# Seeding a PSUM bank with ScalarE's copy of product one instead of adding a snapshot, in a seven-product matmul kernel

## The chip, the cores and the metric

The kernel runs on one core of one Trainium2 chip, in fp32 throughout. The metric is the device time of one execution in microseconds (us). TensorE (PE) does the matmuls and writes PSUM; VectorE (DVE), ScalarE (ACT) and GpSimd (POOL) do the rest; SyncE (SP) issues nearly all DMAs. Each engine works through a queue of its own, in the order in which the built program put its instructions there.

## The reference, cut to what matters

`x` is (8, 512, 512); the feed-forward width is 2048. Linear attention and a gated feed-forward run on the same normalized tokens, and the one gates the other:

```python
xn = layernorm(x)
q, k, v = xn @ Wq.T + bq, xn @ Wk.T + bk, xn @ Wv.T + bv
s = ((elu(q) + 1) * cumsum((elu(k) + 1) * v, axis=1) * 32 ** -0.5) @ Wo.T + bo
h = fwht(xn * SU_ug) / 64                      # Walsh-Hadamard transform
h = silu(h @ W_gate.T * (Wscale_ug[2048:] * 64)) * (h @ W_up.T * (Wscale_ug[:2048] * 64))
y = (fwht(h * SU_dp) / 64) @ W_down.T * (Wscale_dp * 64)
out = x + s * silu(y)
```

## The kernel before, in words

**Seven products for a matmul.** A product of two 2x2 block matrices is made from seven block products instead of eight (Strassen's scheme in Winograd's form), of operands that were added up beforehand (`encode_tokens`, `encode_weights`). The seven are P1 to P7; in the code their indices are `P1, P2, P7, P3, P4, P5, P6 = range(7)`, so a tile called `gu_1_0_3` is pair 1, hidden unit 0, outer product with index 3, which is P3. The four outputs are sums of them, and most of the summing happens in PSUM: bank `px` takes P1, then P6, P5 and P3 onto it; bank `pz` takes P7, then P4. Between the steps a copy of `px` is read away.

- Output 1 = P1 + P2. Before: `px` after P1 is read to SBUF (snapshot `sa`), P2 goes to a bank of its own, `py`, and VectorE adds the two.
- Output 2 = (P1 + P6) + P4 and output 4 = (P1 + P6 + P5) + P7: snapshots `sb` and `sc`, each added to `pz` by VectorE.
- Output 3 = `px` after P3, read directly.

PSUM's eight banks are three `px`, one `py`, two `pz` and two `t` (L447).

**Three recorders** write this order out:

- `group` (L450), for k, v, q (24 times in all) and, in the first pair, gate and up (12 times). A source matmul has 512 columns and shows as two passes; a product has two such matmuls. Snapshots are ScalarE's, with the bias added.
- `token_groups` (L520), for the attention's output projection `o` (4 times) and the down projection `dn` (8 times). It runs two groups of rows, g = 0 and 1, side by side. Where something has to be added (a bias, or the first half of `dn`), the read of `px` is a VectorE addition (L547), else a ScalarE copy (L545).
- `block_product` (L630), for a hidden unit's gate and up together (`gu`), 91 times. This is a second level: a hidden unit is itself seven outer products P1, P5, P6, P2, P7, P3, P4 (`hidden_unit`, L810 on), each a `block_product` of seven inner products of two 128x256 source matmuls. The reads of `px` are plain ScalarE copies for the outer P1 and P5 (L646, L674) and VectorE additions onto an earlier outer result for the others (L648, L676). The addition for output 1 is L657, that of the last inner product L680.

**The order of the work** is written out with an agenda: `at(place, fn)` puts a step at a place, `advance(n)` runs what is due. A `block_product` puts its steps at places 0 P1, 2 P2, 3 P7, 4 P6, 8 P5, 12 P3, 13 P4, and advances by 7, so that the last three fall between the first four of the next block, at its places 1, 5 and 6. The order on PE is therefore P1, previous P5, P2, P7, P6, previous P3, previous P4. `group` does the same with places in units of a product. A scheduler then places the instructions on the engines' queues, waits included, by priority; it can move an instruction of one engine past another where nothing depends on it.

**The stages.** Four pairs p of batch entries: attention (k, v, q for each of two groups of heads), then four hidden units u; `o` follows u = 0, `dn` follows u = 1 (first half) and u = 3 (second half, whose outputs go through Silu, L882, a product on POOL, L883, and an addition, L884). In pair 0 the first three units use `group` with weights that are folded on the chip meanwhile (`folded_w` L946-952, `fold_down` L998-1004), so VectorE and ScalarE have much more to do there; 13 units go through `hidden_unit`: u = 3 of pair 0 and all of pairs 1 to 3.

**The end of a hidden unit.** With outer P7 done, POOL adds its result `r` to `v` in two halves (L842, in `with_r`), ScalarE puts each half through Silu (L828, in `gated`), and POOL multiplies (L829). Outer P3 and P4 follow on PE meanwhile.

Of the kernel before, what the change touches and what calls it, by code (L numbers as in the profile page):

```python
# [8 lines left out]
F32 = mybir.dt.float32  # L9
AF = mybir.ActivationFunctionType  # L10
# [11 lines left out]
def kernel(  # L22
# [66 lines left out]
    def pace(ins, us):  # L89
        while us > 0 and (urgent or idle):  # L90
            t, fn, args = (urgent or idle).pop(0)
            with tc.issue_after(ins.ins):
                fn(*args)
            us -= t
# [24 lines left out]
    su_ug = const.tile([P, KD], F32, tag="su_ug", name="su_ug")  # L119
    su_dp = const.tile([P, NF], F32, tag="su_dp", name="su_dp")  # L120
# [329 lines left out]
    def group(name, ws, rhs, dst, then, bias=(None, None), time=1.7):  # L450

        n = len(ws)
        u = n

        def product(p, i, first):
            for k in range(n):
                r = rhs(k, i)
                nc.tensor.matmul(  # L460
                    p.rearrange("p a t -> p (a t)") if len(r.shape) == 2 else p, ws[k][:, i, :], r,
                    start=(first and k == 0), stop=(k == n - 1), skip_group_check=True,
                )

        def snapshot(what, i):
            s = snap.tile([P, L], F32, tag="s", name=f"{what}_{name}")
            b = bias[min(i, 1)]
            p = px.rearrange("p a t -> p (a t)")
            if b is None:
                nc.scalar.copy(s, p)  # L470
            else:
                nc.scalar.activation(s, p, AF.Identity, bias=b)
            return s

        def output(i, s, p):
            pace(nc.vector.tensor_tensor(dst[i], s, p.rearrange("p a t -> p (a t)"), ALU.add), time)  # L476

        px, py, pz = (bank(t, name, 2) for t in ("px", "py", "pz"))
        sums = {}

        def p1():
            product(px, P1, True)
            sums["a"] = snapshot("sa", 0)

        def p2():
            product(py, P2, True)
            output(0, sums["a"], py)

        def p6():
            product(px, P6, False)  # L490
            sums["b"] = snapshot("sb", 1)

        def p7():
            product(pz, P7, True)

        def p5():
            product(px, P5, False)
            sums["c"] = snapshot("sc", 2)
            output(2, sums["c"], pz)

        def p3():
            product(px, P3, False)

        def p4():
            product(pz, P4, False)
            output(1, sums["b"], pz)
            then(px.rearrange("p a t -> p (a t)"))

        at(0, p1)
        at(u, p2)  # L510
        at(3 * u, p6)
        at(5 * u, p7)
        at(6 * u, p5)
        at(9 * u, p3)
        at(11 * u, p4)
        advance(7 * u)
        between()


    def token_groups(name, n, tok, wts, dst, add=None, early=None, done=None, last=None):  # L520
# [20 lines left out]
        def read(what, o, a, s, g):  # L541
            if o is None:
                o = snap.tile([P, 2, 2 * P], F32, tag="s", name=f"{what}_{name}_{g}")
            if add is None:
                nc.scalar.copy(o, px[g])  # L545
            else:
                pace(nc.vector.tensor_tensor(o, px[g], add(a, s, g), ALU.add), 1.3)  # L547
            return o
# [6 lines left out]
        def p1(g, ks=None):  # L555
            if g not in px:
                px[g] = bank("px", f"{name}_{g}", 2)
            product(px[g], P1, g, True, ks)
            if ks is None or n - 1 in ks:
                sums["a", g] = read("sa", None, 0, 0, g)  # L560
# [12 lines left out]
        def p2(g):  # L573
            py[g] = bank("py", f"{name}_{g}", 2)
            product(py[g], P2, g, True)
            output(sums["a", g], py[g], 0, 0, g)
# [53 lines left out]
    def block_product(name, w, x, out, add, done):  # L630


        px, py, pz = (bank(t, name, 2) for t in ("px", "py", "pz"))
# [16 lines left out]

        def p1():
            product(px, P1, True)
            sums["a"] = read("sa", 0, 0)

        def p2():
            product(py, P2, True)
            nc.vector.tensor_tensor(out[:, 0, :, 0], sums["a"], py, ALU.add)  # L657
# [13 lines left out]
        def p3():  # L671
            product(px, P3, False)
            if add is None:
                nc.scalar.copy(out[:, 0, :, 1], px)  # L674
            else:
                nc.vector.tensor_tensor(out[:, 0, :, 1], px, add[:, 0, :, 1], ALU.add)  # L676
# [7 lines left out]
        for place, fn in ((0, p1), (2, p2), (3, p7), (4, p6), (8, p5), (12, p3), (13, p4)):  # L684
            at(place, fn)
# [6 lines left out]
    def attention(p, xo, co, get_w):  # L692
        def project(m, g, then):
            w = get_w(m, g)
            r = t8.tile([P, 2, 2, L], F32, tag="t", name=f"{m}_{p}_{g}")
            b = (col("b" + m, g), col("b" + m, g + 2))

            def whole(px):
                nc.scalar.activation(r[:, 0, 1], px, AF.Identity, bias=b[0])
                then(r)  # L700

            group(
                f"{m}_{p}_{g}", [w[:, 0], w[:, 1]], x_rhs(xo),
                (r[:, 0, 0], r[:, 1, 0], r[:, 1, 1]), whole, b, 1.7,
            )

        def elu_plus_one(r, name):
            neg = t8.tile([P, 2, 2, L], F32, tag="t", name=f"neg_{name}")
            for h in range(2):
                nc.scalar.activation(neg[:, h], r[:, h], AF.Relu, scale=-1.0)  # L710
                nc.scalar.activation(neg[:, h], neg[:, h], AF.Exp, scale=-1.0)
                nc.vector.scalar_tensor_tensor(r[:, h], r[:, h], 1.0, neg[:, h], ALU.add, ALU.max)

        def heads(g):
            phi = {}

            def with_k(k):
                phi["k"] = k
                elu_plus_one(k, f"k_{p}_{g}")

            def with_v(v):
                k = phi["k"]
                for h in range(2):
                    nc.vector.tensor_tensor(v[:, h], v[:, h], k[:, h], ALU.mult)
                    at(4 + 4 * h, lambda h=h: sums(k, v, h))

            def sums(k, v, h):
                for s in range(2):
                    nc.vector.tensor_tensor_scan(
                        k[:, h, s], ones.to_broadcast([P, L]), v[:, h, s], 0.0, ALU.mult, ALU.add  # L730
                    )

            def with_q(q):
                k = phi["k"]
                elu_plus_one(q, f"q_{p}_{g}")
                for h in range(2):
                    nc.vector.scalar_tensor_tensor(  # L737
                        co[:, g, h : h + 3 : 2, :], k[:, h], QSCALE, q[:, h], ALU.mult, ALU.mult
                    )
                encode_tokens(nc.gpsimd, co[:, g])  # L740

            project("k", g, with_k)
            project("v", g, with_v)
            project("q", g, with_q)

        for g in range(2):
            heads(g)
# [31 lines left out]
    def gate(p, f, xo, get_w):  # L779
        w = get_w("gate", f)  # L780
        g = t8.tile([P, 2, 2, L], F32, tag="t", name=f"g_{p}_{f}")

        def with_gate(px):
            nc.scalar.activation(g[:, 0, 0], g[:, 0, 0], AF.Silu, scale=col("w_gate", f))
            nc.scalar.activation(g[:, 0, 1], px, AF.Silu, scale=col("w_gate", f))
            nc.scalar.activation(g[:, 1], g[:, 1], AF.Silu, scale=col("w_gate", f + NG))

        group(
            f"gate_{p}_{f}", [w[:, 0], w[:, 1]], x_rhs(xo),
            (g[:, 0, 0], g[:, 1, 0], g[:, 1, 1]), with_gate,  # L790
        )
        return g

    def up(p, f, g, xo, ho, get_w, last):

        w = get_w("up", f)
        r = t8.tile([P, 2, 2, L], F32, tag="t", name=f"u_{p}_{f}")

        def with_up(px):
            nc.gpsimd.tensor_tensor(ho[:, P1], g[:, 0, 0], r[:, 0, 0], ALU.mult)  # L800
            nc.vector.tensor_tensor(ho[:, P7], g[:, 0, 1], px, ALU.mult)
            nc.gpsimd.tensor_tensor(ho[:, P2 : P3 + 1 : 2], g[:, 1], r[:, 1], ALU.mult)
            encode_tokens(nc.vector if last else nc.gpsimd, ho)

        group(
            f"up_{p}_{f}", [w[:, 0], w[:, 1]], x_rhs(xo),
            (r[:, 0, 0], r[:, 1, 0], r[:, 1, 1]), with_up,
# [333 lines left out]
    for i in range(7):  # L1141
# [5 lines left out]
        src = dst  # L1147
    xo = xop.tile([P, 7, 7, H], F32, tag="xo", name="xo_0")
# [4 lines left out]
    nc.vector.tensor_scalar(su_ug, col("su_ug", 0, KD), D ** -0.5, None, ALU.mult)  # L1153
    nc.vector.scalar_tensor_tensor(
# [149 lines left out]
```

## Time and profile before

| | |
|---|---|
| median of 3 runs | 1551.32 us (1550.75 to 1551.83) |
| profiled execution, span of its instructions | 1552.4 us |
| PE busy | 1523.8 us, 98% |
| VectorE busy | 1002.4 us, 65% |
| ScalarE busy | 418.9 us, 27% |
| GpSimd busy | 436.7 us, 28% |
| granted TensorE clock, mean | 0.998 |

The profile comes from one execution, 1.1 us above the median of the runs. Its timeline gives each instruction's start and duration in us from the span's start, with the idle time of the engine before it and what ended that in brackets; runs of equal instructions are joined with their count (x8). A source matmul shows as two passes, so a `gu` step of two source matmuls is x4 and takes 0.864 us from start to start (216 ns each), and a product of `group` is four passes of 432 ns, 1.73 us. The views of waits and of groups by line give totals over the execution.

### The profile page before, as it was taken

What the parts mean: (1) busy time and instruction counts of PE and PEld (TensorE: products, weight loads), DVE (VectorE), ACT (ScalarE), POOL (GpSimd) and SP (SyncE); (2) the same over time, 40 slices, a digit from 0 to 9 for tenths busy, and PEclk for the clock granted to TensorE, in tenths of its full rate; (3) what the DMA queues carried; (4) which work ended last, traced back from release to release, by engine and by line L of the source; (5) the groups of instructions that cost most, each with busy time, mean ns of one, the idle gap of its engine ahead of it and who ended that gap; (6) DMA issues with size and microseconds to landing.
All of it is one profiled execution on the core that took longest, in us unless ns stands there. A gap on an engine that the chain in (4) does not pass through costs nothing.

```text
span 1552.4 us, 15693 instructions
## 1 busy us (share of the span) xinstructions
PE 1523.8 (98%) x5924; PEld 1121.3 (72%) x5924; DVE 1002.4 (65%) x1423; ACT 418.9 (27%) x664; POOL 436.7 (28%) x236
## 2 busy tenths in 40 slices
PE   7989999999999999999999999999999999999998
PEld 3436446746874588888884488888886478888887
DVE  7989787378867665516767674715675575533673
ACT  4452341141125411112114431111213431111211
POOL 1232233004320261205511144302621126210631
PEclk9999999999999999999999999999999999999999
DMA  8345877687985244354576344335574233535462
GB/s 276 98 141 176 258 250 240 214 276 261 267 283 162 90 154 160 95 166 164 166 265 235 93 143 149 114 119 186 175 245 155 87 112 102 191 100 174 164 258 81
DMA packets 197692, 273.31 MB, mean 176 GB/s; under 512 B 56816, under 2 KB 155120, under 8 KB 193392
## 3 DMA queue, kind: packets, MB, share of 16 engines
q1 hardware_dynamic: 197472, 272.27, 54.0%
q8 instruction: 47, 0.77, 0.2%
q14 instruction: 29, 0.24, 0.0%
q10 hardware_dynamic: 144, 0.03, 0.0%
HBM read 196.25 MB, written 76.02 MB: 175 GB/s over the span
## 4 chain that ended last, share of the span: by engine, by line
PE 90%; DVE 6%; DMA 1%; ACT 1%; issue 1%; SPq 0%; POOL 0%; POOLq 0%; DVEq 0%; ACTq 0%
PE px_gu L638 20%; PE px_dn L536 13%; PE pz_gu L638 10%; PE pz_dn L536 6%; PE py_gu L638 5%; PE px_k L460 4%; PE py_dn L536 4%; PE px_o L536 3%; PE px_v L460 3%; PE px_q L460 3%; PE px_up L460 2%; PE pz_o L536 2%; PE pz_k L460 2%; PE pz_v L460 2%; PE pz_q L460 2%; PE px_gate L460 1%
## 5 line engine op out<-in xcount | busy, mean ns | idle before, releaser
L638 PE MATMUL px_gu<-xo,w_gu 128*128 128x256 f32 x1456 | 347.7, 380 | 1.4 <-DVE sb_gu L648 1.4
L638 PEld LDWEIGHTS px_gu<-xo,w_gu 128*128 128x128 f32 x1456 | 275.7, 190 | 45.9 <-issue 5.0
L536 PE MATMUL px_dn<-w_down,ho 128*128 128x256 f32 x1024 | 228.7, 379 | 0.0
L536 PEld LDWEIGHTS px_dn<-w_down,ho 128*128 128x128 f32 x1024 | 194.6, 190 | 28.6 <-issue 2.4
L638 PE MATMUL pz_gu<-xo,w_gu 128*128 128x256 f32 x728 | 187.7, 380 | 1.1 <-DVE u L476 1.1
L838 POOL TENSOR_TENSOR u<-u,v 128x1024 f32<-128x1024 f32 x26 | 61.0, 2367 | 365.9 <-DVE u L676 347.4
L638 PEld LDWEIGHTS pz_gu<-xo,w_gu 128*128 128x128 f32 x728 | 137.5, 190 | 22.3 <-DVE u L476 1.5
L536 PE MATMUL pz_dn<-w_down,ho 128*128 128x256 f32 x496 | 112.5, 379 | 1.7 <-DVE u L476 1.7
L536 PEld LDWEIGHTS pz_dn<-w_down,ho 128*128 128x128 f32 x496 | 93.7, 190 | 16.4 <-DVE u L476 2.1
L638 PE MATMUL py_gu<-xo,w_gu 128*128 128x256 f32 x364 | 93.4, 379 | 0.0
L304 POOL TENSOR_TENSOR co<-co 128x512 f32<-128x512 f32 x8 | 14.6, 1829 | 266.3 <-DVE co L737 266.3
L883 POOL TENSOR_TENSOR s<-s,d 128x512 f32<-128x512 f32 x30 | 40.0, 1333 | 165.4 <-ACT d L882 165.4
L638 PEld LDWEIGHTS py_gu<-xo,w_gu 128*128 128x128 f32 x364 | 69.2, 190 | 9.4
L842 POOL TENSOR_TENSOR v<-v,r 128x1024 f32<-128x1024 f32 x26 | 60.9, 2361 | 26.9 <-DVE r L676 26.9
L460 PE MATMUL px_k<-xo,w_k 128*128 128x512 f32 x128 | 61.8, 606 | 0.0
L460 PE MATMUL px_v<-xo,w_v 128*128 128x512 f32 x128 | 60.6, 594 | 0.0
L460 PE MATMUL px_q<-xo,w_q 128*128 128x512 f32 x128 | 60.3, 592 | 0.0
L828 ACT ACTIVATE a<-a,cols_sb 128x512 f32<-128x512 f32 x26 | 18.7, 721 | 149.5 <-DVE a L676 147.8
L882 ACT ACTIVATE d<-d 128x512 f32<-128x512 f32 x31 | 19.5, 630 | 144.4 <-DVE d L551 124.7
L536 PE MATMUL px_o<-w_o,co 128*128 128x256 f32 x256 | 58.2, 379 | 0.0
L828 ACT ACTIVATE u<-u,cols_sb 128x512 f32<-128x512 f32 x52 | 36.9, 720 | 78.2 <-DVE u L676 75.0
L536 PE MATMUL py_dn<-w_down,ho 128*128 128x256 f32 x256 | 57.9, 379 | 0.0
(269 smaller groups left out, 2417.4 us busy)
## 6 DMA issues: line engine op xcount, KB each, us to landing
w_gu<-d_gu SPq DMA_DIRECT2D x91, 896.0 KB, 4.5
w_down<-d_down SPq DMA_DIRECT2D x56, 512.0 KB, 3.8
d_s<-o SPq DMA_DIRECT2D x8, 1024.0 KB, 5.7
d_d<-dn SPq DMA_DIRECT2D x8, 1024.0 KB, 7.7
d<-d_d SPq DMA_DIRECT2D x8, 1024.0 KB, 6.3
s<-d_s SPq DMA_DIRECT2D x8, 1024.0 KB, 8.1
y<-in_x_dram SPq DMA_DIRECT2D x8, 1024.0 KB, 6.4
out_dram<-y SPq DMA_DIRECT2D x15, 512.0 KB, 3.2
```

Source lines behind the costliest of these rows:

```text
L304: eng.tensor_tensor(o[..., P5, :], o[..., P7, :], o[..., P1, :], ALU.subtract)
L460: nc.tensor.matmul(p.rearrange("p a t -> p (a t)") if len(r.shape) == 2 else p, ws[k][:, i, :], r, start=(first and k == 0), stop=(k == n ...
L536: nc.tensor.matmul(p[:, c], t[:, (2 * g + c) * P : (2 * g + c + 1) * P], ws[i](k), start=(first and k == 0 and c == cs[0]), stop=(k == n - ...
L638: nc.tensor.matmul(p[:, lane], w[:, lane, i, :], x[:, i, :], start=(first and lane == 0), stop=True, skip_group_check=True,)
L828: nc.scalar.activation(g[:, m], g[:, m], AF.Silu, scale=col("w_gate", u + m * NU + a * NG))
L838: nc.gpsimd.tensor_tensor(r[:, m], ru1[:, m], rv[:, m], ALU.add)
L842: nc.gpsimd.tensor_tensor(rv[:, m], rv[:, m], rr[:, m], ALU.add)
L882: nc.scalar.activation(d, d, AF.Silu)
L883: (nc.vector if final and (a, s) == (1, 0) else nc.gpsimd).tensor_tensor(r, r, d, ALU.mult)
```

## The change

In every group of seven products, the read of `px` after P1 no longer goes to SBUF. ScalarE copies it into the bank `py` (PSUM to PSUM, a new helper `seeded`), and P2 is accumulated onto it with `start=False`. Output 1 is then in `py` and is read from there by whatever uses it first; VectorE's addition L476, L551 or L657 falls away, or becomes the addition that the snapshot had done. One identity matmul over the whole of `py` stands at the start of the program (`all_written`), ahead of the first seed.

- `block_product`: seeding copy after P1, always ScalarE's, also where the snapshot was a VectorE addition. Output 1 is `final(py, 0, 0)`: a ScalarE copy for outer P1 and P5, one VectorE addition for the others. P7 and P2 change places (P7 at 2, P2 at 3).
- `token_groups`: the same, with the seed of g = 1 in a third `px` bank, so that both groups can be under way.
- `group`: P2 moves from place u to 2u, P3 from 9u to 8u (u = 2 is one product). For k and q the first quarter of elu reads the bank with the bias in the instruction (new constants `neg_b`, `b_plus_one`; four small VectorE operations at the start), quarter by quarter instead of half by half; v's first quarter is weighted straight from the bank; the gate's first Silu and the up projection's first multiplication (POOL before, L800, VectorE now) read it too.

The core of the diff:

```diff
+    def all_written():
+        p = bank("py", "first", 4)
+        nc.tensor.matmul(p, ident, ident.unsqueeze(1).to_broadcast([P, 4, P]), start=True, stop=True)
+
+    def seeded(px, tag, name):
+        p = bank(tag, name, px.shape[1])
+        nc.scalar.copy(p, px)
+        return p
...
# group
         def p1():
             product(px, P1, True)
-            sums["a"] = snapshot("sa", 0)
+            sums["a"] = seeded(px, "py", f"py_{name}")
         def p2():
-            product(py, P2, True)
-            output(0, sums["a"], py)
+            product(sums["a"], P2, False)
+            pace(first(flat_bank(sums["a"])), time)
...
-        at(u, p2)
+        at(2 * u, p2)
...
-        at(9 * u, p3)
+        at(8 * u, p3)
...
# token_groups
             if ks is None or n - 1 in ks:
-                sums["a", g] = read("sa", None, 0, 0, g)
+                py[g] = seeded(px[g], ("py", "px")[g], f"py_{name}_{g}")
...
         def p2(g):
-            py[g] = bank("py", f"{name}_{g}", 2)
-            product(py[g], P2, g, True)
-            output(sums["a", g], py[g], 0, 0, g)
+            product(py[g], P2, g, False)
+            read("", dst(0, 0, g), 0, 0, g, py[g])
...
# block_product
+        def final(p, m, q):
+            if add is None:
+                nc.scalar.copy(out[:, m, :, q], p)
+            else:
+                nc.vector.tensor_tensor(out[:, m, :, q], p, add[:, m, :, q], ALU.add)
+
         def p1():
             product(px, P1, True)
-            sums["a"] = read("sa", 0, 0)
+            sums["a"] = seeded(px, "py", f"py_{name}")
         def p2():
-            product(py, P2, True)
-            nc.vector.tensor_tensor(out[:, 0, :, 0], sums["a"], py, ALU.add)
+            product(sums["a"], P2, False)
+            final(sums["a"], 0, 0)
...
-        for place, fn in ((0, p1), (2, p2), (3, p7), (4, p6), (8, p5), (12, p3), (13, p4)):
+        for place, fn in ((0, p1), (2, p7), (3, p2), (4, p6), (8, p5), (12, p3), (13, p4)):
             at(place, fn)
...
# attention
+        def elu_of_bank(r, neg, x, m, g):
+            nc.scalar.activation(neg, x, AF.Relu, bias=neg_b[m][:, g : g + 1], scale=-1.0)
+            nc.scalar.activation(neg, neg, AF.Exp, scale=-1.0)
+            return nc.vector.scalar_tensor_tensor(r, x, b_plus_one[m][:, g : g + 1], neg, ALU.add, ALU.max)
...
+            def weighted(v, s, x):
+                return nc.vector.scalar_tensor_tensor(
+                    v[:, 0, s], x, col("bv", g), phi["k"][:, 0, s], ALU.add, ALU.mult
+                )
...
# up
-            nc.gpsimd.tensor_tensor(ho[:, P1], g[:, 0, 0], r[:, 0, 0], ALU.mult)
+        def first(py):
+            return nc.vector.tensor_tensor(ho[:, P1], g[:, 0, 0], py, ALU.mult)
```

## Prediction

> **What bounds the kernel now.** I read the busy times first, then the slices, then PE's waits.
>
> ```profile
> PE 1523.8 (98%) x5924; PEld 1121.3 (72%) x5924; DVE 1002.4 (65%) x1423; ACT 418.9 (27%) x664; POOL 436.7 (28%) x236
> ```
>
> PE is busy 1523.8 of 1552.4 us, so the matmul stream is the bound, and what the other engines do counts only where a matmul waits. Cut by stage (busy us of PE, PEld, DVE, ACT, POOL, with instruction counts; then clock, DMA share, GB/s):
>
> ```profile
> 0.00:100.00 100.00, 90.09 (x222) 41.26 (x223) 91.93 (x150) 46.27 (x80) 22.88 (x27) 1.00 0.54 171
> 100.00:200.00 100.00, 95.06 (x276) 51.91 (x275) 85.44 (x102) 40.62 (x94) 32.15 (x18) 1.00 0.69 214
> 300.00:390.00 90.00, 84.46 (x253) 47.92 (x252) 67.58 (x111) 26.03 (x45) 20.98 (x13) 0.98 0.81 261
> 460.00:640.00 180.00, 180.00 (x672) 126.71 (x671) 118.03 (x162) 56.69 (x75) 54.26 (x27) 1.00 0.45 143
> ```
>
> From 460 us on PE does not pause (180.00 of 180.00). Its pauses lie in the first 390 us, where weights are folded and VectorE is 92% and 85% busy. Their causes (engine, line, who was waited for: us in total, times, longest):
>
> ```profile
> PE pt L271 <- ACT x L178: 7.5, 1, 7.5
> PE pwd L998 <- ACT w_gate L952: 3.7, 1, 3.7
> PE pw_gate L946 <- DVE r_gate L940: 2.2, 1, 2.2
> ...
> PE pz_dn L536 <- DVE u L476: 1.7, 1, 1.7
> PE px_gu L638 <- DVE sb_gu L648: 1.4, 1, 1.4
> PE pz_gu L638 <- DVE u L476: 1.1, 1, 1.1
> ```
>
> The first is the start, untouched. Waits for VectorE sum to 2.2 + 1.7 + 1.4 + 1.1 and three smaller ones of 0.8, 0.7, 0.5: 8.4 us. That is all a relief of VectorE can win.
>
> **Part 1: work moved.** Every group loses one VectorE addition (L657: 680 ns, x91; L551 687, L476 684) and gains a ScalarE copy where the snapshot was not ScalarE's already. The nearest row is the same copy into SBUF (line, engine, operation, tile; busy us and mean ns; idle before it):
>
> ```profile
> L646 ACT COPY sa_gu<-px_gu 128x512 f32<-128x512 f32 x26 | 15.1, 581 | 80.0 <-PE px_gu L638 80.0
> ```
>
> VectorE loses some 150 x 0.68 = 100 us and ScalarE gains 60 to 90 us. Neither is a term: after 390 us VectorE's time is hidden beside a PE that never pauses. PE itself does the same passes; P2 accumulates in place of starting. The copy into PSUM is shown by no row. Below, 0.43 us is an estimate: (687 - 472) ns over 256 elements between the activations L472 (128x512) and L952 (128x256) is 0.84 ns an element, so 512 take 0.43 us with no fixed cost left. Above I take 1.17, twice the row. I use 0.585, the row of the same size, source and operation.
>
> [...]
>
> **Part 2: what the copy stands behind.** Before, the reader of P2 joined snapshot and `py` at leisure; now P2's matmul itself waits for the seed, so PE depends on ScalarE 91 + 36 + 24 times. The question is what stands ahead of each seed on ScalarE. In a `block_product` PE runs P1, previous P5, P7, P2: P1 ends two steps, 1.73 us, before P2 is due. A reader starts about 0.2 us after the matmul, the copy takes 0.585, release takes about 0.1 (sa_k ended at 460.42, the px_k matmul behind it began at 460.51): 0.9 of 1.73, so 0.8 us to spare when ScalarE is free.
>
> It is not free at the end of a hidden unit. In the order of the changed program, all 12 units of pairs 1 to 3 have on ScalarE: seed of outer P3, Silu of v's first half, **seed of outer P4**, Silu of v's second half. That first Silu waits for POOL. The timeline of before, one such place:
>
> ```profile
> 629.55 0.69 DVE L676 TENSOR_TENSOR r<-px_gu,u 128x512 f32<-128x512 f32 x1
> ...
> 630.21 1.89 PE L638 MATMUL px_gu<-xo,w_gu 128*128 128x256 f32 x8
> 630.39 4.68 POOL L842 TENSOR_TENSOR v<-v,r 128x1024 f32<-128x1024 f32 x2 [2.14 <-DVE r L676]
> ...
> 631.28 0.69 DVE L648 TENSOR_TENSOR sa_gu<-px_gu,r 128x512 f32<-128x512 f32 x1 [0.18 <-PE px_gu L638]
> ...
> 631.94 1.03 PE L638 MATMUL py_gu<-xo,w_gu 128*128 128x256 f32 x4
> ...
> 632.78 0.72 ACT L828 ACTIVATE v<-v,cols_sb 128x512 f32<-128x512 f32 x1 [6.96 <-POOL v L842]
> 632.80 1.03 PE L638 MATMUL pz_gu<-xo,w_gu 128*128 128x256 f32 x4
> ```
>
> The row 630.21 is outer P4's P1 and the previous P5. VectorE read P1 at 631.28 (`sa_gu`), with no Silu in its way. In the changed kernel the seed has to wait for the Silu that idled 6.96 us and began at 632.78: it ends at 633.50, the seed at 634.09, P2 can start at 634.18. P2 is due as the fourth step, 630.21 + 3 x 0.864 = 632.80. **PE stands 1.4 us.** POOL's start is fixed by the last `r` of outer P7, which waits for PE (629.35 + 0.2), so a lighter VectorE does not move it. The same gap from the Silu's start to P2's due time is there in all 12 units within 0.03 us, but in the last, where POOL starts 0.3 us later. Sum: 11 x 1.4 + 1.7 = 17.1 us. PE later by 1.4 us gives the seeds that follow more room, not less. In the unit of pair 0 the seed stands ahead of both Silu: nothing.
>
> Nothing was lost there before, though the wait was long (totals of the waits view):
>
> ```profile
> ACT v L828 <- POOL v L842: 110.6, 26, 7.3
> ```
>
> 110.6 us of waiting cost nothing, because nothing that PE needed stood behind it.
>
> The next tightest: outer P3's seed behind the two Silu of a, and the next unit's first seeds behind the two Silu of u3 and of u1. From the timeline (Silu u1 about 733.95 to 734.67, seed to 735.26, P2 due at 735.62) 0.2 to 0.3 us are left. I cost them at 0; if the copy takes 1.17, about 30 such places miss by 0.3, some 10 us.
>
> **Part 3: start of attention, pairs 1 to 3.** The group of k stands behind the last Silu of `dn`:
>
> ```profile
> 457.07 1.88 PE L460 MATMUL px_k<-xo,w_k 128*128 128x512 f32 x4
> ...
> 458.50 0.68 DVE L551 TENSOR_TENSOR d<-sb_dn,pz_dn 128x512 f32<-128x512 f32 x1
> 458.79 1.88 PE L460 MATMUL py_k<-xo,w_k 128*128 128x512 f32 x4
> ...
> 459.21 0.63 ACT L882 ACTIVATE d<-d 128x512 f32<-128x512 f32 x1 [3.07 <-DVE d L551]
> ```
>
> Seed from 459.84 to 460.43; P2 at 460.52. In the changed program one matmul of P7 (0.86 us) fits between, so P2 is due at 458.79 + 0.86 = 459.65: 0.87 us lost. Then Relu and Exp of the bank (0.69 each) with a table load (1.28, row L711) stand ahead of `sb_k`, which ends near 465.8 where PE wants it at about 465.7: 0.1 to 0.4. Together 1.2 x 3 = 3.5 us.
>
> **Part 4: small things.** After `o`, `dn` and attention no previous block fills P1 to P2, so P2 is due one step after P1: at 596.47 it would be due at 598.19, the copy L646 ended at 598.11, released 598.20. About 0.05 x 9 = 0.5 us. At the start, the four small operations stand ahead of the first layernorm statistics (rows like it pitch 0.08 us apart: +0.1), and the Relu of k's bank stands ahead of the last copy of transposed x: I take 0.5 to 1.5. In steady attention ScalarE has 56.69 busy of 180 us, seeds come early enough. Elsewhere in pair 0, both ways are open: folds on ScalarE (387 and 472 ns each) stand ahead of seeds, VectorE is relieved. Bounds -8.4 (all its waits gone) and, by two or three stalls of the size of the present ones, +6; I take -0.5, near nothing, since the largest present waits (7.5, 3.7) are for ScalarE.
>
> **Sum.** 17.1 + 3.5 + 0.5 + 1.0 - 0.5 = 21.6. The profiled 1552.4 would become 1574; its place above the median (1.1 us) is left as it is, so the median goes from 1551.3 to **1573**.
>
> [...] The cost of the alternative first, from rows: a seed through PE would be two passes of 0.432 us, 0.86 x 151 = 130 us. [...]
>
> **The rivals.**
> - *Faster.* If the v Silu is not what the seed waits for, only VectorE's relief remains, in the first 390 us: down to 1551.3 - 8.4 = 1543. For it: VectorE 92% busy there. Against it: the order on ScalarE. It decides if the stalls in outer P4 come to under 8.4 / 12 = 0.7 us, that is if POOL's half addition ended 0.7 us sooner than its 2.36. Chance 0.07.
> - *No change.* The blockade costs half of my sum (8.5 us) and pair 0 wins back its whole bound of 8.4: 1549 to 1554. Chance 0.06.
> - *Partly.* The blockade costs half, or pair 0 gains most of its bound, not both: 1555 to 1566. Chance 0.10.
> - *Seeds miss in more places.* The copy into PSUM takes twice the row: 12 x 0.585 = 7 on the blockade, 10 on the tight places: 1590. For it: no row shows such a write. Chance 0.12.
> - *The forecast*, 1566 to 1580: 0.65.
>
> The range leaves out the faster and unchanged cases and the far end of the last but one: 1556 to 1586. A measurement of this kernel can tell about 0.2% from no change; faster 0.07, within it 0.06, slower 0.87.
>
> **What would show it.** In the changed profile, ScalarE's group of seeds should have idle time ended by PE only, but outer P4's `py_gu` matmuls in pairs 1 to 3 should wait about 1.4 us for ScalarE's seed, with Silu v directly ahead of the seed; 12 waits of that length. PE's waits for ScalarE should sum to some 20 us more; VectorE's busy time should fall by about 100 us. The seed copy's mean tells part 1's unknown. I am wrong if PE runs through outer P4 without a pause, if the seed's mean is above 0.8 us, or if pair 0's stretch (0 to 390 us) moves by more than 6 us.

## The result and the profile after

| | before | after |
|---|---|---|
| median of 5 runs each, same chip | 1551.32 us | 1597.88 us (1595.51 to 1599.59) |
| ratio, 95% interval | | 1.0295 [1.0283, 1.0308] |
| profiled span | 1552.4 us | 1596.0 us |

The change costs 2.95%, 46.6 us by the medians and 43.6 us by the two profiles. (A run's time here is 1.7 to 2.1 us above the span in its profile, so the profile of before is of an execution some 2.9 us above the median of the runs, an estimate from 1552.4 + 1.8 - 1551.3; the 1.1 us told ahead compare a span with a time. Delays by the profiles can be too small by as much.) The forecast was 1573 with a range to 1586: the direction was right, the size half of what came.

The busy row of the changed kernel, and its rows of the seeds and of the matmuls that follow them in `block_product` (busy us and mean ns; idle before, and what ended it):

```profile
PE 1539.3 (96%) x5926; PEld 1124.0 (70%) x5926; DVE 923.1 (58%) x1306; ACT 475.2 (30%) x787; POOL 409.4 (26%) x230
L462 ACT COPY py_py_gu<-px_gu 128x512 f32<-128x512 f32 x91 | 52.2, 573 | 189.7 <-PE px_gu L655 189.6
L655 PE MATMUL py_py_gu<-xo,w_gu 128*128 128x256 f32 x364 | 94.8, 383 | 9.7 <-ACT py_py_gu L462 9.7
```

VectorE lost 79 us of work and ScalarE gained 56, as the change means to, and the time rose all the same. PE's busy time rose by 15.5 us with two instructions more, so PE also ran slower somewhere (mean granted clock 0.991, before 0.998). Its waits say where it stood (us in total, times, longest):

```profile
PE px_dn L551 <- DMA w_down<-d_down: 10.4, 1, 10.4
PE py_py_gu L655 <- ACT py_py_gu L462: 9.7, 9, 1.1
PE py_py_k L477 <- ACT py_py_k L462: 7.0, 3, 2.9
PE pt L275 <- ACT x L182: 4.5, 2, 4.3
PE pwd L1034 <- ACT rd L1040: 3.2, 3, 1.4
PE pw_gate L982 <- DVE r_gate L976: 2.4, 1, 2.4
PE pt L275 <- ACT xo L279: 2.3, 1, 2.3
PE px_up L477 <- issue: 2.2, 1, 2.2
```

To place the loss in time I compared when both kernels had done the same number of matmul columns (the table gives times of the changed kernel; wherever a delay "at" a time is told further on, the time is that of the kernel before):

| where (us in the changed kernel) | lost, us |
|---|---|
| pair 0, to 394 us | 16.9 |
| - of that: 139 to 157 (the bank that `up` needs is read late) | 6.5 |
| - of that: 217 to 267 (the first load of `w_down`) | 14.4 |
| - of that: the rest, both signs | -4.0 |
| nine places in outer P4, pairs 1 to 3 | 12.5 |
| three starts of attention, pairs 1 to 3 (5.2, 5.1, 2.0) | 12.3 |
| steps of 0.3 to 0.4 (unit starts and the like) | 1.9 |

**One of the nine places**, in the timeline of the changed kernel (start, duration; idle before in brackets):

```profile
653.78 1.89 PE L655 MATMUL px_gu<-xo,w_gu 128*128 128x256 f32 x8
653.95 4.67 POOL L878 TENSOR_TENSOR v<-v,r 128x1024 f32<-128x1024 f32 x2 [2.12 <-DVE r L672]
...
656.35 0.72 ACT L864 ACTIVATE v<-v,cols_sb 128x512 f32<-128x512 f32 x1 [6.48 <-POOL v L878]
...
656.98 0.58 ACT L462 COPY py_py_gu<-px_gu 128x512 f32<-128x512 f32 x1
...
657.61 1.13 PE L655 MATMUL py_py_gu<-xo,w_gu 128*128 128x256 f32 x4 [1.07 <-ACT py_py_gu L462]
```

The seed's source was ready by about 655; ScalarE stood idle for 6.48 us, but before an instruction that waited for POOL. P2 came 1.24 us after its due time of 656.37 (653.78 + 3 x 0.864), and what followed it 1.34 late.

**A start of attention**, same columns:

```profile
479.92 0.63 ACT L918 ACTIVATE d<-d 128x512 f32<-128x512 f32 x1 [2.89 <-DVE d L567]
480.46 0.58 ACT L462 COPY py_py_k<-px_k 128x512 f32<-128x512 f32 x1
...
481.09 3.63 PE L477 MATMUL py_py_k<-xo,w_k 128*128 128x512 f32 x4 [2.84 <-ACT py_py_k L462]
...
484.52 1.97 PE L477 MATMUL px_k<-xo,w_k 128*128 128x512 f32 x4
```

The same trap at another place, and a second cost behind it: after the idle 2.84 us the four passes took 3.63 us, where four such passes take 1.97 three microseconds later. The stretch of these four (columns as in the next block) shows a granted clock of 0.54:

```profile
481.00:484.50 3.50, 3.41 (x4) 1.37 (x5) 0.69 (x1) 0.04 (x1) 0.90 (x1) 0.54 1.03 382
```

**The wait for `w_down`**, by stretches (busy us of PE, PEld, DVE, ACT, POOL with counts; then clock, DMA share, GB/s):

```profile
256.80:260.00 3.20, 0.00 (x0) 0.00 (x0) 3.17 (x7) 0.00 (x0) 0.00 (x0) 0.50 0.59 156
260.00:264.00 4.00, 3.29 (x8) 2.66 (x9) 3.04 (x4) 0.00 (x0) 0.00 (x0) 0.50 1.05 344
264.00:266.50 2.50, 2.50 (x8) 2.03 (x7) 1.53 (x2) 0.00 (x0) 0.00 (x0) 0.55 0.80 234
266.50:270.00 3.50, 3.50 (x17) 3.07 (x17) 1.09 (x1) 0.00 (x0) 0.00 (x0) 1.00 1.04 273
```

PE stands until 260.71, then runs at a granted clock of 0.50 to 0.55 until 266.5: 8 passes in 3.29 busy us where 17 take 3.50 afterwards.

**The bank that `up` needs**, in the timeline again, and by stretches behind it:

```profile
145.95 2.36 DVE L1015 TENSOR_TENSOR rd<-rd 128x1024 f32<-128x1024 f32 x2
148.22 0.69 DVE L563 TENSOR_TENSOR o<-px_py_o,bo_r 128x512 f32<-128x512 f32 x1
...
149.01 2.60 PE L477 MATMUL px_up<-xo,w_up 128*128 128x512 f32 x4 [2.21 <-issue]
...
150.00:153.00 3.00, 2.34 (x4) 0.64 (x3) 3.00 (x7) 0.57 (x1) 0.00 (x0) 0.53 0.00 0
153.00:156.00 3.00, 3.00 (x7) 1.84 (x6) 1.41 (x3) 0.00 (x0) 0.00 (x0) 0.50 0.54 154
```

`token_groups` now keeps a third `px` bank until VectorE has read output 1 from it; that read (148.22, ending 148.91) stands behind a fold's additions, and PE's next `px` starts 0.1 us after it. The view names "issue", since it saw no releaser: that PE waits for this bank is read from the order of the rows, and no run shows it. (With `token_groups` alone, which keeps the bank as well, only 0.1 us is lost in this stretch.) The pause is 2.2 of the 6.5 us; behind it the granted clock was 0.53 and 0.50 for six us.

### The profile page after: what moved, and what is told of

Its sections match the earlier page's. It is cut to its first block, busy times and chain, and to the rows that moved or that the text cites. A ratio compares the mean times of both kernels' runs of the same rounds, so it can differ in the third digit from the quotient of the medians.

```text
span 1596.0 us, 15737 instructions
## 1 busy us (share of the span) xinstructions
PE 1539.3 (96%) x5926; PEld 1124.0 (70%) x5926; DVE 923.1 (58%) x1306; ACT 475.2 (30%) x787; POOL 409.4 (26%) x230
## 4 chain that ended last, share of the span: by engine, by line
PE 81%; DVE 8%; POOL 3%; issue 3%; DMA 3%; ACT 2%; POOLq 0%; SPq 0%; DVEq 0%; ACTq 0%
PE px_gu L655 18%; PE px_dn L551 9%; PE pz_gu L655 8%; PE pz_dn L551 5%; PE py_py_gu L655 5%; PE px_o L551 4%; PE px_q L477 3%; PE px_v L477 3%; PE px_k L477 3%; PE px_up L477 3%; PE px_gate L477 2%; PE pz_o L551 2%; PE py_py_dn L551 2%; POOL v L878 2%; PE pz_v L477 2%
## 5 line engine op out<-in xcount | busy, mean ns | idle before, releaser
L551 PE MATMUL px_dn<-w_down,ho 128*128 128x256 f32 x1024 | 232.1, 383 | 10.6 <-DMA w_down<-d_down 10.4
L551 PEld LDWEIGHTS px_dn<-w_down,ho 128*128 128x128 f32 x1024 | 196.2, 192 | 41.1 <-DMA w_down<-d_down 11.3
L551 PE MATMUL pz_dn<-w_down,ho 128*128 128x256 f32 x496 | 112.1, 379 | 0.0
L462 ACT COPY py_py_gu<-px_gu 128x512 f32<-128x512 f32 x91 | 52.2, 573 | 189.7 <-PE px_gu L655 189.6
L655 PE MATMUL py_py_gu<-xo,w_gu 128*128 128x256 f32 x364 | 94.8, 383 | 9.7 <-ACT py_py_gu L462 9.7
L551 PEld LDWEIGHTS pz_dn<-w_down,ho 128*128 128x128 f32 x496 | 94.2, 190 | 12.8
L655 PEld LDWEIGHTS py_py_gu<-xo,w_gu 128*128 128x128 f32 x364 | 67.9, 190 | 23.7 <-ACT py_py_gu L462 14.6
L308 POOL TENSOR_TENSOR co<-co 128x512 f32<-128x512 f32 x8 | 11.1, 1389 | 248.8 <-DVE co L772 135.0
L551 PE MATMUL px_o<-w_o,co 128*128 128x256 f32 x256 | 59.6, 386 | 0.0
L308 POOL TENSOR_TENSOR ho<-ho 128x512 f32<-128x512 f32 x5 | 7.2, 1435 | 197.6 <-DVE ho L838 197.6
```

The source lines that it names most:

```text
L308: eng.tensor_tensor(o[..., P5, :], o[..., P7, :], o[..., P1, :], ALU.subtract)
L462: nc.scalar.copy(p, px)
L551: nc.tensor.matmul(p[:, c], t[:, (2 * g + c) * P : (2 * g + c + 1) * P], ws[i](k), start=(first and k == 0 and c == cs[0]), stop=(k == n - ...
L655: nc.tensor.matmul(p[:, lane], w[:, lane, i, :], x[:, i, :], start=(first and lane == 0), stop=True, skip_group_check=True,)
```

## The experiments

Other chips ran the kernel before at 1553.8 to 1556.2 us, so ratios to it on the same chip are compared. Delays at a place compare profiles of different chips, and can be some us off. The theory at this point: **ScalarE's queue** (a seed stands behind an instruction that waits) makes the nine places and the starts of attention, and something else makes pair 0's loss. The rivals: the seeds themselves are slow, the added ScalarE work is what costs, or everything comes from one of the three recorders.

**One recorder at a time.** Each has the identity matmul and `seeded`, and the change in one recorder alone:

```diff
# e1_block_only: block_product; e2_group_only: group and what calls it; e3_token_only: token_groups
+    all_written()
```

> Only the recorder of the hidden units (block_product, 91 seeds) is changed, with the identity matmul at the start; group and token_groups are those of before. Theory A (a few places, each with something slow ahead of the seed on ScalarE): nine stalls of about 1.4 us ahead of outer P4's P2 and a few tenths at unit starts, some 13 us: 1564 to 1567 us, and no long wait for down weights at 250 us. Rival B (every seed costs PE a little, whatever stands ahead): 91 of 151 seeds of 46.5 us, 28 us: about 1579.

> Only group (k, v, q, gate, up) is changed; block_product and token_groups are those of before. Theory A: about 1 us at the start and 12 us at the three starts of attention, 1563 to 1566 if the late down weights in pair 0 do not come from here; 1575 to 1582 if they do (a wait of some 10 us at about 250 us and a TensorE clock of half for some microseconds behind it). Rival B: 36 of 151 seeds, 11 us: 1562.

> Only token_groups (o and dn) is changed; group and block_product are those of before. Theory A: 1551 to 1554 alone, since no wait of PE for a seed was seen in o and dn; 1562 to 1570 if the down weights in pair 0 become late through this recorder, which no longer hangs paced work on the read after P1. Rival B: 24 of 151 seeds, 7 us: 1559.

Measured: 1.0130 [1.0108, 1.0151], 1.0049 [1.0032, 1.0065] and 1.0115 [1.0098, 1.0133]. On the scale of 1551.3 us these are 1571.5, 1558.9 and 1569.1: the first is 4.5 us above its theory's range, the second below both of its ranges, the third in the range for late weights, and none where a small cost of every seed would put it. They sum to 2.94%, as much as the change; since each holds the identity matmul and its own order of pair 0, this does not show that the parts add. From PE's waits, of the first and then of the third:

```profile
PE py_py_gu L649 <- ACT py_py_gu L458: 9.6, 9, 1.1
```

```profile
PE px_k L471 <- ACT sa_k L483: 4.7, 3, 2.1
...
PE px_dn L547 <- DMA w_down<-d_down: 3.4, 1, 3.4
```

The nine waits belong to `block_product` alone. With `group` alone a start of attention costs 0.8 + 0.4 us, what the prediction had worked out for it (1.2). `token_groups` alone, in which k still has its snapshot, costs 2.3, 2.3 and 0.8 there, because the last Silu of `dn` runs later: at the first start 4.4 us after k's P1, as in the changed kernel, where it was 2.1 before and with `group` alone. A layernorm of the next input now stands ahead of it on ScalarE and VectorE. `token_groups` also brings the largest share of pair 0's loss (11.1 us at 383 us; `block_product` alone 5.6 at 387, `group` alone 3.9 at 383). So the starts of attention are two recorders' work: `group` puts PE behind the Silu, `token_groups` makes the Silu late.

**Undo the head of the queue.** The changed kernel, with the Silu of v put behind outer P4's seed on ScalarE:

```diff
+                with nullcontext() if behind is None else tc.issue_after(behind.ins):
+                    nc.scalar.activation(g[:, m], g[:, m], AF.Silu, scale=col("w_gate", u + m * NU + a * NG))
-            gated(rv, 1, 1, nc.gpsimd)
+            at(4, lambda: gated(rv, 1, 1, nc.gpsimd, last_seed[0]))
```

> The changed kernel, with one edit: the two Silu of v stand behind the seed of outer P4 on ScalarE. Theory A: the nine waits of about 1.1 us of outer P4's P2 go, 12 us less than the changed kernel: 1584 to 1587. Rival (the Silu is not what the seed waits for, or the wait moves to the next seed): 1595 or more.

Measured: 1.0191 [1.0173, 1.0209], 1.04% better than the change (span 1581.9, 14 us less; 1580.9 on the scale of the forecast, which had 1584 to 1587). Its first waits, with the one of `py_py_gu` gone from its place between them:

```profile
PE px_dn L553 <- DMA w_down<-d_down: 10.7, 1, 10.7
PE py_py_k L479 <- ACT py_py_k L464: 7.0, 3, 2.8
```

Every seed is still copied by ScalarE, with as much work. Only the place of the Silu in the order (and of the POOL product that follows it) is edited, so order was the cause of these nine waits, and neither the copy's length nor the added load.

**The same for the start of attention**: the last Silu of `dn` of pairs 0 to 2 behind the seed of the next k.

```diff
+            if half == 1 and not final and (a, s, g) == (1, 0, 1):
+                left_over.append(lambda: gated_now(a, s, g, last_seed[0]))
+            else:
+                gated_now(a, s, g)
```

> The changed kernel, with one edit: the last Silu of dn in pairs 0 to 2 stands behind the next k's seed on ScalarE. Theory A: the waits of k's P2 (2.8, 2.9 and 1.3 us, and the half clock of some 2 us behind the first two) go, 8 to 10 us less than the changed kernel: 1587 to 1590 where that runs at 1597.9. Rival (P2 waits for something else, or for the Silu before): no change.

Measured: 1.0253 [1.0238, 1.0268], span 1591.9. The waits for k are gone, and another has come:

```profile
PE py_py_gu L660 <- ACT py_py_gu L465: 9.6, 9, 1.1
...
PE px_v L480 <- ACT sc_v L490: 3.5, 2, 1.8
```

By the spans some 4 of 12 us come back (6.5 by the ratios, at the edge of the forecast). Now v's snapshot is late: on ScalarE it stands behind the Relu of k's second half, which waits 5.15 us for VectorE. Whether the moved Silu causes this is not shown; in the run with three edits further on, with the same Silu moved, this wait of PE is 0.3 us. A start of attention is tight for several instructions of ScalarE.

**Pair 0: give the background its anchors back.** Folding weights, adding up operands and their DMAs are background work, recorded by `pace` after instructions of the main stream. The change takes the read of `sa` from `token_groups`, and with it two portions from each call. In the changed profile the second layernorm result of the next pair is stored at 243.7 us, against 223.6 before; the additions that make `s_gate` follow at 249.2 against 227.8, and the first `w_down`, whose buffer still holds weights that they read, is issued at 257.0 against 233.7 (before, then after):

```profile
233.71 2.31 SPq L339 DMA_DIRECT2D w_down<-d_down  x2
...
257.01 0.34 SPq L343 DMA_DIRECT2D w_down<-d_down  x1
```

This edit hangs the missing portions on the seed:

```diff
+                if add is not None:
+                    pace(last_seed[0], 1.3)
```

> The changed kernel, with one edit: the seed of token_groups, where the snapshot was an addition with paced work hung on it, gets that paced work hung on it again. Theory A (o gives out two portions of paced work fewer, so the folds of the down weights, the layernorm of the third input and the stores behind it run 8 to 20 us later, and the down weights' first load waits behind those stores on SP): the wait of 10.4 us at about 250 us falls to under 3, with the half clock behind it, 10 to 15 us less: 1583 to 1588. Rival (the lateness comes from group, whose P2 comes later): the wait stays above 8 us.

Measured: 1.0248 [1.0233, 1.0263], span 1590.5. The 10.4 us are gone from the waits, and others stand in their place:

```profile
PE pz_o L553 <- DVE g L493: 6.1, 1, 6.1
PE pw_gate L986 <- DVE r_gate L980: 4.3, 2, 2.4
```

At 377 us the delay is 16.2 instead of 16.9: pair 0 has gained next to nothing, and on the forecast's scale the time is 1589.8, above its range. The first `w_down` is still issued at 250.6 us, 17 us later than before; PE, itself 11 us late by 237 us, waits 1.0 us for it. With `group` alone, whose `token_groups` is the earlier one, it is issued at 246.4. So the lost anchors are at most a part of its lateness, and do not explain pair 0's loss. What this kernel gained came after 400 us.

**The three edits together.**

> The changed kernel with the three edits together (Silu of v behind the seed, last Silu of dn behind the seed, paced work given back). Theory A: the three gains add up, 30 to 37 us less than the changed kernel: 1561 to 1568. Rival (each wait has another behind it that ends nearly as late): 1575 or more.

Measured: 1.0144 [1.0127, 1.0161], or 1573.7 us, between the theory and its rival: the gains do not add up. Behind 377 us only about 5 us are lost; up to there, in pair 0, 16.9.

**The first `w_down` in a buffer of its own** (taken from the snapshots' pool, 4 buffers instead of 6), alone and with the two Silu edits:

```diff
+        if name == ("down", (0, P1)) and not first_down:
+            first_down.append(own.tile([P, 4, 2 * P], F32, tag="fd", name="first_down"))
+            nc.sync.dma_start(first_down[0], wd[0][:, P1])
+            return first_down[0]
```

> The changed kernel, with one edit: the first load of down weights in pair 0 goes to a buffer of its own (the snapshots' pool shrinks from 6 to 4 to make room), so it waits neither for the weight buffer that the late s_gate additions still read nor for their stores. Theory A (the down weights were made in time, by 215 us, and the load alone was held up by the buffer): the wait of 10.4 us shrinks to at most 4 for the loads after the first, with no half clock: 6 to 12 us less than the changed kernel, 1586 to 1592 where that runs at 1597.9. Rival (the additions behind it are late as such, and whatever needs them next stops PE): the wait moves to the second product's weights and 2 us or less are won.

> The changed kernel with Silu of v behind the seed, the last Silu of dn behind the seed, and the buffer of its own. Theory A: gains of about 13, 4 and 6 to 12 us add up: 1570 to 1577. Rival: 1578 or more.

Measured: 1.0248 [1.0233, 1.0264] and 1.0123 [1.0106, 1.0140], or 1589.8 and 1570.4 us, both in the theory's ranges, though the load's wait is longer than the 4 us expected. The second load is now the late one, at half the price:

```profile
PE pz_dn L557 <- DMA w_down<-d_down: 5.5, 1, 5.5
```

At 377 us the delay is 11.4, so the wait for a buffer was worth some 5.5 us of pair 0's 17.

**Is pair 0's loss the change's at all?** Three kernels. First, the kernel before with nothing but the identity matmul:

```diff
+    all_written()
```

> The kernel before, with nothing added but the identity matmul over py at the start. Theory A: it moves the order of the transposes' copies on ScalarE, PE starts on products about 1.2 us later, and two or three more are lost and won back by 110 us: 1552 to 1554. Rival (it is hidden ahead of the first data, as I predicted): within 0.2 us of the kernel before.

Measured: 1.0014 [1.0002, 1.0026]. It is one matmul, and in its profile `pt` waits 2.3 us for ScalarE's copies of transposed x at the start, where it waited 0.8. (By the ratio it loses 2.2 us, by the profiles 6.9, the largest such disagreement here: the profiled execution was the slowest of ten, 3.5 us above their median.) Second, a kernel that keeps the earlier recorders for pair 0 (up to its last hidden unit, and without the identity matmul), and has the change with both Silu edits in the rest:

> Pair 0's k, v, q, gate, up, o and first half of dn use the recorders of before (no identity matmul is needed then); everything else is the changed kernel with the two edits on Silu. Theory A (outside pair 0 only the things behind which the seeds stood cost time; pair 0's loss comes from the order of its background work): 2 to 6 us above the kernel before, 1553 to 1558 where that runs at 1551.3. Rival (the seeds cost more even with nothing slow ahead of them): 1562 or more. The change's own promise (less VectorE work gains something) would show as faster than before, which I expect of no run.

Measured: 1.0125 [1.0110, 1.0140], or 1570.7 us, where 1553 to 1558 had been expected. The expectation missed, and the rival's number (1562 or more) came; but at 358 us, just ahead of its first block product with a seed, this kernel is 5.2 us late already, in a stretch whose code is the earlier one. It is 10 to 12 us late from 377 us on and 19.6 at the end. By the disagreement above, all of the 5.2 could come from the executions compared; the next kernel decides.

```profile
PE pz_dn L733 <- DVE u L561: 4.2, 1, 4.2
PE px_gate L545 <- DVE w_gate L317: 3.9, 2, 2.6
```

The code is the same but the built order is not. The four constants that the later pairs need are four more instructions on VectorE at the start, and the scheduler puts everything after them differently. The third kernel is the one before with these four instructions alone, whose results nothing reads:

```diff
+    for m in ("q", "k"):
+        nc.vector.tensor_scalar(neg_b[m], col("b" + m, 0, KD), -1.0, None, ALU.mult)
+        nc.vector.tensor_scalar(b_plus_one[m], col("b" + m, 0, KD), 1.0, None, ALU.add)
```

> This is the kernel before with nothing of the change but its four small constants: two negated and two raised copies of the biases of q and k (128x4 each, four VectorE instructions at the start), which nothing reads here. The order that is built from it for pair 0 is, on every engine, the one of the run that kept the earlier recorders for pair 0, up to that run's first block product with a seed (at about 300 us); it differs from the order before from the 17th row of TensorE on. Theory A, the delay in pair 0 is mostly the order: small changes at the start reshuffle the order of the first 360 us, which the kernel before had in a good state. Then this kernel shows most of the +12 us that the other run had at 363 us, a ratio of 1.004 to 1.008 (+6 to +12 us), with the same waits of TensorE in pair 0 (px_gate behind VectorE's w_gate, pz_dn behind VectorE's u), and no more after 363 us. Theory B, the delay in pair 0 comes from the changed instructions themselves: then these four, some 0.1 us each and read by nothing, cost nothing, and the ratio is 1.000 to 1.001. In between (1.002 to 1.004) part is the order, and the rest of the +12 us is the new recorders' in pair 0's second half and the difference between chips.

(The 12 us of this expectation were reached at 377 us; at 363 it was 6.2.) Measured: 1.0052 [1.0038, 1.0066], 8 us; by the profile 4.4 us late at 363 us and 9.2 at 387, and no more later. Up to 397 us it stays within some 5 us of the run with the earlier recorders, mostly within 2. Up to 360 us every engine works in the order of that run, while PE's order leaves that of the kernel before at its 51st matmul. Its waits:

```profile
PE pz_dn L540 <- DVE u L480: 4.6, 1, 4.6
PE pz_up L464 <- DVE u L480: 3.1, 1, 3.1
PE px_gate L464 <- DVE w_gate L317: 2.8, 1, 2.8
```

Four instructions that do next to nothing cost as much as six of the nine blockades. What they change is the order in which pair 0's instructions stand on the queues; the `pz_dn` and `px_gate` waits are those of the run with the earlier recorders, while the kernel before waits 1.7 and 0.7 us at the same two. Pair 0 of the kernel before runs in a good order, and two small edits to its start lost some of it (0.14% and 0.52%).

## Why the prediction was right and wrong

- **What bounds the kernel: right.** PE's stream is the bound, and 79 us less on VectorE (forecast: some 100) won nothing that shows.
- **Part 1, work moved: right.** The copy into PSUM takes 573 ns; I had used 585, from the copy into SBUF (581 to 585 in the rows of `gu`): 8 to 12 ns less, which decides nothing. ScalarE gained 56 us, where I had 60 to 90. No run here puts a seed through PE, so the 130 us of the prediction stay an estimate; what ScalarE's seeds cost here is queue order, not the copy.
- **Part 2, the blockade: right in mechanism and in the size of one, wrong in the count.** 1.34 to 1.46 us each, 1.4 forecast; the Silu edit makes them vanish. But there are nine, not twelve: 12.5 us for 17.1. In the units u = 0, the built program has the last P3 of outer P7's group ahead of the next group's P2, so `r` is done sooner and POOL starts at 585.41, 1.57 us before the row of outer P4's P1; in the place shown it starts 0.17 after that row. I had read twelve equal gaps from the trace of before, whose order on PE the change does not keep.
- **Part 3, start of attention: mis-sized, 12.3 us for 3.5.** My working holds for `group` alone (0.8 + 0.4 measured, 1.2 forecast). It took the end of `dn`'s last Silu from the trace of before, though `token_groups` is changed as well and makes that Silu later (4.4 us after k's P1, for 2.1). And behind PE's pause at two of three starts the granted clock was 0.54, which costs some 1.7 us more (3.63 for 1.97).
- **Part 4, elsewhere in pair 0: the step that failed.** I took -0.5 with bounds of -8.4 and +6; it was +16.9 at 377 us, outside the bound, which the prediction itself had named as a sign of being wrong. I had bounded it by the waits present before, as if the order stayed and only durations changed. The runs show three things in its place: the order of pair 0 is shuffled by small edits at its start (9.2 us by the profile for four instructions that nothing reads); background work comes late, at the worst 10.4 us of waiting for one load (5.5 us back when it has a buffer of its own; the reads that the work hung on are a part of the reason at most); and time at a granted clock of 0.50 to 0.55 behind some of the pauses. How the 17 us divide between these is not settled: the parts don't add, since each edit also reshuffles the order (giving the anchors back removed one wait and brought another of 6.1). A kernel with the change and pair 0's order exactly as before was not built.
- **The start and the unit starts.** +1.0 at 25 us, in my 0.5 to 1.5; what makes it is not shown. With the identity matmul alone PE's first product starts 1.9 us later (15.51 for 13.59), since ScalarE's copies of transposed x come later, but at 25 us nothing of that is left (-0.1). The small steps came to 1.9 for 0.5.
- **The rivals.** "Faster" fell at its own point: the stalls are 1.4 us, not under 0.7. "Seeds miss in more places" (1590) came nearest in time, but its reason was wrong and the nearness luck: the copy was not slow. What was missing among the rivals was the order of the work itself.

No kernel run here beats the one before. The best of those that keep all seeds, with both Silu edits and `w_down`'s own buffer, is at 1.0123.

## What to carry to other kernels

Before an engine in the bottleneck's path takes over a step, list for every place what stands ahead of it on that engine's queue and what that waits for, in the order of the new program; a long wait that costs nothing today can become a stall once something urgent stands behind it (here 110.6 us of ScalarE's waiting for POOL had cost nothing, and nine stalls of 1.34 to 1.46 us came of it). Durations and gaps taken from the old trace hold only where nothing that feeds them is changed. Where a scheduler fixes the order and a stage is full, measure an edit that does nothing beside the one that matters: here one cost 0.5%, and a gain or loss of that size says little about the idea.

## What the runs showed of the hardware

**The clock after a pause.** Behind some of PE's pauses the granted clock was 0.50 to 0.55 for some 3 to 6 us, which a waits view does not count. In the kernel before, PE pauses 2.24 us by the profile and the four passes behind the pause take longer:

```profile
258.96 1.88 PE L946 MATMUL pw_gate<-r_gate,had 128*128 128x512 f32 x4
...
304.93 2.45 PE L946 MATMUL pw_gate<-r_gate,had 128*128 128x512 f32 x4 [2.24 <-DVE r_gate L940]
307.17 3.13 PE L460 MATMUL px_gate<-xo,w_gate 128*128 128x512 f32 x4
...
306.30:308.00 1.70, 1.70 (x3) 0.62 (x2) 0.59 (x1) 1.19 (x4) 0.00 (x0) 0.50 0.96 274
```

The row 258.96 is four such passes without a pause: 1.88 us. Behind the pause they take 2.45 and the next four 3.13, and the last row, a stretch as above, has a granted clock of 0.50. After the changed kernel's pauses of 2.21 us (0.53 and 0.50), 2.84 us (x4 in 3.63 at 0.54) and 10.43 us (0.50 to 0.55 for some 6 us) the same; after its pause of 1.33 at the third start of attention it did not happen (x4 in 1.98 at 1.00). Nor is the length of the pause alone what decides: after the changed kernel's pause of 2.36 us at 321.27 four passes took 1.95 at a granted clock of 1.00, and in the run with the four constants a pause of 3.06 us ahead of 371.81 was followed by four passes in 1.98. In these rows a granted clock of about half came behind pauses of 2.21 us and more, but not behind each of them. What decides whether the clock drops stays open.
